# Layer 0 cross attention without wide GpSimd work, pair attention with sums from columns of ones, layer norms on ScalarE

## The chip, the cores and the metric

The kernel runs on one core of a Trainium2 chip. The metric is the device time of one execution in microseconds (us). A core has five engines that run side by side and meet through semaphores: TensorE (PE in the profile, its weight loads PEld), VectorE (DVE), ScalarE (ACT), GpSimd (POOL) and SyncE (SP), which issues most DMAs. Each engine takes its own instructions in order.

## The reference, cut to what matters

A four-layer network on x of shape (16, 64, 256), so 1024 tokens of 256 features, with a context of (16, 1601, 256). Each layer has a cross attention, a self attention and a feed forward block, each on a layer norm of x and added to x. The change touches three of the twelve blocks and every norm.

```
def _layernorm(x, axis=-1, eps=1e-05):
    m = jnp.mean(x, axis=axis, keepdims=True)
    v = jnp.var(x, axis=axis, keepdims=True)
    return (x - m) / jnp.sqrt(v + eps)
...
x = x + _L0_xattn_ref(_layernorm(x, axis=-1), ctx_1024, ctx_1024, mask)
x = x + _L0_attn_ref(_layernorm(x, axis=-1), ...)
...
x = x + _L1_attn_ref(_layernorm(x, axis=-1), ...)
```

Layer 0 cross attention has 16 heads of 16 features over 1601 keys, with a mask that is added to the scores, and a softmax. Layer 0 self attention has 16 heads of 16 over the 64 tokens of a batch element, causal, with a softmax. Layer 1 self attention is linear attention with a feature map elu + 1: its weights are products of q and k, masked causally, and each row is divided by its sum plus 1e-6.

## The kernel before, in words

x stays in SBUF as eight tiles of 128 tokens (two batch elements each); `xn` holds its layer norm. The twelve blocks are the stages of `run`, one after the other. A Tile scheduler orders the instructions of each engine, except those that `pinned` keeps in the order in which the program writes them (while `self.fixed` is set). Weights of the next stage and the context are fetched on SP's queue.

**Norms.** Wherever a tile of x is finished, `ready(t)` runs: L299 and L301 compute mean and variance on VectorE, L303 adds the epsilon on VectorE, L304 takes the power -0.5 on GpSimd. `normalise`, called for the tile before at the next `ready` and once more at the end of a stage, writes xn on VectorE (L311, 128x256). There are 96 of each in a run. In several stages `add_bias` (L350, GpSimd, 128x256) then adds an output bias to x, once xn has been read from it.

**Layer 0 cross attention.** The work is cut into 32 units: 16 batch elements, each with two halves kc of the features (eight heads). A unit has four chunks of 384, 384, 384 and 449 keys. A step n of the main loop does `scores` of one chunk, `lower` of the chunk four steps back, `values` of the chunk six back and `turn` of the chunk five back. `scores`: four matmuls `s` of 32 rows each, into four single-buffered PSUM banks, and on VectorE four L447 that add the mask `mneg`, keep a running maximum and write `Sx`. After the fourth chunk L454 and L457 give the maximum m and its negative. `lower` subtracts m from the four planes of `Sx`: two planes on VectorE (L470), one on ScalarE (L465), one on GpSimd (L466). `turn` transposes them on TensorE (L199, three PSUM buffers `pst`) and takes the exponential on ScalarE (L491; L484 for the 65 keys of the tail, in the last chunk). `values` multiplies by the context with a column of ones into `acc`. `prepare(b)` for the next batch element runs in the first step of each second unit: it issues the context and the mask DMAs, turns the mask from uint8 to -10000 on GpSimd (L419, 128x1601) and masks q on VectorE (L423). Once in two batch elements `back` transposes and divides, and `ready` follows.

**Self attention of layers 0 and 1.** `pair_values` computes V for each tile with V's head columns spread with zeros: 64 x 64-token matmuls, one for each half of the partitions, and L917 adds the bias. The attention loop over eight tiles is a pipeline: `scores` (matmuls into `S4`, then VectorE; in layer 0 also L1037 on GpSimd and an exponential), in layer 0 `turn`, then `values`, then `out`. `values` calls `pair_attend`: 16 matmuls with V as the stationary side give the attention transposed, 8 matmuls with the constant `own` give each head's sum repeated over 32 partitions, a reciprocal of 128x256 on VectorE (L1094, L1092), and a product L1096 that gives `aT`. `out` projects aT (`py`), adds to x (L357) and calls `ready`.

Of the kernel before, what the change touches and what calls it, by code (L numbers as in the profile page):

```python
# [8 lines left out]
F32 = mybir.dt.float32  # L9
# [7 lines left out]
P = 128  # L17
# [27 lines left out]
def _constants():  # L45
# [21 lines left out]
    put("par", ((p[:, None] // 16) % 2) == np.arange(2)[None, :])  # L67
    put("half", (p[:, None] // S) == np.arange(2)[None, :])
    put("iota8", np.broadcast_to(np.arange(8), (P, 8)))
    put("pow", np.broadcast_to(np.array([-0.5, 0.5]), (P, 2)))  # L70
    put("cadd", np.where(same & (p[None, :] <= p[:, None]), 0.0, -1.0e30))
    put("own", (p[:, None] // S) == (np.arange(32)[None, :] // 16))
    put("cadd64", np.where(np.arange(S)[None, :] <= p[:, None] % S, 0.0, -1.0e30))
    put("hd8", ((p[:, None] // 16) == np.arange(8)[None, :]) / S)
    put("neg1", -np.ones((P, 1)))
# [98 lines left out]
class Net:  # L174
# [119 lines left out]
    def ready(self, t):  # L294


        nc, x = self.nc, self.x[:, t, :]
        st = self.stat.tile([P, 6], F32, tag="bst", name="bst")
        nc.vector.bn_stats(st, x)  # L299
        mv = self.stat.tile([P, 2], F32, tag="mv", name="mv")  # L300
        nc.vector.bn_aggr(mv, st)  # L301
        rs = self.stat.tile([P, 1], F32, tag="rs", name="rs")
        nc.vector.tensor_scalar(rs, mv[:, 1:2], 1e-5, None, ALU.add)  # L303
        nc.gpsimd.tensor_tensor(rs, rs, self.c("pow")[:, 0:1], ALU.pow)  # L304
        self.normalise()
        self.due = t, mv, rs

    def normalise(self):
        if self.due is not None:
            t, mv, rs = self.due  # L310
            self.nc.vector.tensor_scalar(  # L311
                self.xn[:, t, :], self.x[:, t, :], mv[:, 0:1], rs, ALU.subtract, ALU.mult
            )
            self.due = None

# [74 lines left out]
    def L0_xattn(self, _):  # L390
# [4 lines left out]
        with (  # L395
# [5 lines left out]
            with (  # L401
# [8 lines left out]
                units = [(b, kc) for b in range(B) for kc in range(2)]  # L410
                state, pairs = {}, {}

                def prepare(b):
                    cn, cT = self.load_ctx(b, "ctx_ones")
                    m8 = sp.tile([P, S2], U8, tag="m8", name="m8", bufs=1)
                    nc.sync.dma_start(m8[0:S], self.io["mask0"][b])
                    nc.sync.dma_start(m8[S:P], self.io["mask0"][b])
                    mneg = sp.tile([P, S2], F32, tag="mneg", name="mneg")
                    nc.gpsimd.tensor_scalar(mneg, m8, -10000.0, 1.0, ALU.mult, ALU.mult)  # L419

                    q = sp.tile([P, 2, 2, S], F32, tag="q", name="q")
                    for i in range(2):
                        nc.vector.tensor_scalar(  # L423
                            q[:, :, i, :], xnT[:, :, b * S : (b + 1) * S],
                            self.c("hm2")[:, i : i + 1], None, ALU.mult,
                        )
                    for kc in range(2):
                        state[2 * b + kc] = dict(b=b, kc=kc, cn=cn, cT=cT, mneg=mneg, q=q, S=[])

                def scores(u, c):  # L430

# [20 lines left out]
                    if c == 3:  # L452
                        m = small.tile([P, 4], F32, tag="m", name="m")
                        nc.vector.tensor_reduce(m, st["mx"], AX.X, ALU.max)  # L454
                        st["m"] = m
                        st["neg"] = small.tile([P, 1], F32, tag="neg", name="neg")
                        nc.vector.tensor_scalar(st["neg"], m[:, 2:3], -1.0, None, ALU.mult)  # L457

                def lower(u, c):

                    st = state[u]
                    n = CHUNKS[c][1]
                    Sj = [st["S"][c][:, j, :n] for j in range(4)]
                    m = st["m"]
                    self.pinned(nc.scalar.activation(Sj[2], Sj[2], AF.Identity, bias=st["neg"]))  # L465
                    nc.gpsimd.tensor_tensor(  # L466
                        Sj[3], Sj[3], m[:, 3:4].to_broadcast([P, n]), ALU.subtract
                    )
                    for j in range(2):
                        self.pinned(nc.vector.tensor_scalar(  # L470
                            Sj[j], Sj[j], m[:, j : j + 1], None, ALU.subtract
                        ))
# [68 lines left out]


                N = 4 * len(units)
                prepare(0)
                for n in range(N + 9):
                    if n < N:
                        scores(*divmod(n, 4))
                        if n % 8 == 4 and n // 8 + 1 < B:
                            prepare(n // 8 + 1)
                    if 0 <= n - 4 < N:  # L550
                        lower(*divmod(n - 4, 4))
                    if 0 <= n - 6 < N:
                        values(*divmod(n - 6, 4))
                    if 0 <= n - 5 < N:
                        turn(*divmod(n - 5, 4))
                    t, i = divmod(n - 7, 16)
                    if i == 15 and t >= 0:
                        back(t)
                    t, i = divmod(n - 8, 16)
                    if i == 15 and t >= 0:  # L560
                        self.ready(t)
# [335 lines left out]
    def pair_values(self, pool, pp, xT, w, bias):  # L897


        nc = self.nc  # L900
        n, k = w.shape[1], xT.shape[0]
        V = pool.tile([P, B, 8, 2, 16], F32, tag="V", name="V")
        nc.gpsimd.memset(V, 0.0)
        bias = bias.rearrange("p (a i f) -> p a i f", i=2, f=16)
        for t in range(NT):
            ps = self.psum(pp, [P, 2, 8, 2, 16], "pst")
            for i in range(2):
                b = 2 * t + i
                for kc in range(n):
                    for r in (slice(0, S), slice(S, P)):  # L910
                        self.mm(
                            ps[r, i].rearrange("p a i f -> p (a i f)"),
                            xT[:, kc, b * S : (b + 1) * S], w[:k, kc, :], kc == 0, kc == n - 1,
                        )
            for i in range(2):
                r = slice(i * S, (i + 1) * S)
                self.pinned(nc.vector.tensor_tensor(  # L917
                    V[r, 2 * t : 2 * t + 2, :, i, :], ps[r, :, :, i, :],
                    bias[r, :, i, :].unsqueeze(1).to_broadcast([S, 2, 8, 16]), ALU.add,
                ))  # L920
        return V.rearrange("p b a i f -> p b a (i f)")

    def L0_attn(self, w):

        nc, tc = self.nc, self.tc
# [1 line left out]
        with (  # L929
# [78 lines left out]
            with (  # L1008
# [42 lines left out]
                    state[t] = PT  # L1051

                def values(t):
                    state[t] = self.pair_attend(sp, psa, V, state[t], t, 0.0)

                def out(t):
                    py = self.psum(psa, [P, D], "py")
# [1 line left out]
                        self.mm(py, state[t][:, kc, :], wo[:, kc, :], kc == 0, kc == 1)  # L1059
                    self.finish_x(t, py)  # L1060

                for n in range(NT + 4):
                    if n < NT:
                        scores(n)
                    if 0 <= n - 4 < NT:
                        out(n - 4)
                    if 0 <= n - 3 < NT:
                        values(n - 3)
                    if 0 <= n - 2 < NT:
                        turn(n - 2)  # L1070
                self.fixed = False

    def pair_attend(self, sp, psa, V, PT, t, eps):


        nc = self.nc
        acc = self.psum(psa, [P, 2, 2, P], "acc")
        for kc in range(2):
            for b in range(2):
                for j in range(4):  # L1080
                    self.mm(
                        acc[32 * j : 32 * j + 32, 0, kc, b * S : (b + 1) * S],
                        V[:, 2 * t + b, 4 * kc + j, :], PT[:, 2 * j + kc, b * S : (b + 1) * S],
                    )
            for j in range(4):
                self.mm(
                    acc[32 * j : 32 * j + 32, 1, kc, :], self.c("own"), PT[:, 2 * j + kc, :]
                )
        rec = sp.tile([P, 2, P], F32, tag="rec", name="rec")
        if eps:  # L1090
            self.pinned(nc.vector.tensor_scalar(rec, acc[:, 1], eps, None, ALU.add))
            self.pinned(nc.vector.reciprocal(rec, rec))  # L1092
        else:
            self.pinned(nc.vector.reciprocal(rec, acc[:, 1]))  # L1094
        aT = sp.tile([P, 2, P], F32, tag="aT", name="aT")
        self.pinned(nc.vector.tensor_tensor(aT, acc[:, 0], rec, ALU.mult))  # L1096
        return aT

    def elu1_T(self, sp, out, ps, bias, shape):
# [11 lines left out]
    def L1_attn(self, w):  # L1111
# [6 lines left out]
        with tc.tile_pool(name="l1a", bufs=1) as wk:  # L1118
# [32 lines left out]
            with (  # L1151
# [24 lines left out]
                    state[t] = A.rearrange("p j (c b) q -> p (j c) (b q)", b=2)  # L1176

                def values(t):
                    state[t] = self.pair_attend(sp, psa, V, state[t], t, 1e-6)

                def out(t):
                    py = self.psum(psa, [P, D], "py")
# [1 line left out]
                        self.mm(py, state[t][:, kc, :], wout[:, kc, :], kc == 0, kc == 1)  # L1184
                    self.finish_x(t, py)

                for n in range(NT + 2):
                    if n < NT:
                        scores(n)
                    if 0 <= n - 2 < NT:  # L1190
                        out(n - 2)
                    if 0 <= n - 1 < NT:
                        values(n - 1)
                self.fixed = False
# [937 lines left out]
```

## Time and profile before

| | |
|---|---|
| time, median of 3 runs | 3475.49 us (3474.08 to 3479.93) |
| the profiled execution, its own time | 3481.06 us |
| its span, first to last instruction | 3479.3 us |
| mean granted TensorE clock | 0.942 |
| TensorE, VectorE, ScalarE, GpSimd busy | 3170.8, 1387.8, 1065.1, 470.1 us |
| layer 0 cross attention | up to about 558 us |
| layer 0 self attention | about 558 to 657 us |
| layer 1 self attention | about 1856 to 1950 us |

The stage limits are read from the lines that write x at a stage's end (L536 at 557.56, L304 at 656.79, L357 at 1855.52 and 1949.52). The profiled execution is one run with the profiler on, 5.6 us above the median of the runs without it. Busy time is that of an engine's instructions; TensorE's matmuls overlap, and a matmul that is held up inside a group can make the group look longer, so a busy TensorE is not one at its peak.

### The profile page before, as it was taken

The page shows a single profiled execution, that of the slowest core. Times are in us where ns is not written, and L with a number is a line of the kernel's source. Part 1 is how long each engine was busy: PE and PEld are TensorE (multiplying, and loading weights), DVE is VectorE, ACT ScalarE, POOL GpSimd, SP SyncE. Part 2 cuts the span into 40 slices and gives each one's busy share as a digit, 9 for nine tenths or more (in the row PEclk, how much of TensorE's full clock was granted, in tenths as well). Part 3 has the DMA queues.
Part 4 walks back from the last instruction along what each step waited for, and adds up shares of the span by engine and source line. Part 5 has one row for each costly group of instructions (what it writes and reads, how often), then busy time and mean ns, then how long its engine had stood idle before and what let it go on. Part 6 is the DMA issues. An engine that isn't in the chain of part 4 may idle for free.

```text
span 3479.3 us, 69200 instructions
## 1 busy us (share of the span) xinstructions
PE 3170.8 (91%) x29623; PEld 2365.5 (68%) x29623; DVE 1387.8 (40%) x3702; ACT 1065.1 (31%) x2191; POOL 470.1 (14%) x478
## 2 busy tenths in 40 slices
PE   7999998699899999999998689999987978888798
PEld 4666664499566666666665367777766966767697
DVE  6888885622333333333334862222234010126300
ACT  3555654111112111212111112222221367753111
POOL 2333222222100000000000000000001311110132
PEclk9999998699899999999998699999997979998899
DMA  6333331389011112111139001111114835520297
GB/s 198 103 126 124 94 115 58 122 289 320 17 58 56 57 57 76 38 60 55 57 113 308 15 13 57 57 57 57 38 53 162 273 123 179 187 88 1 107 324 246
DMA packets 178368, 395.12 MB, mean 114 GB/s; under 512 B 11446, under 2 KB 142270, under 8 KB 165214
## 3 DMA queue, kind: packets, MB, share of 16 engines
q1 hardware_dynamic: 165070, 372.81, 31.2%
q0 software_dynamic: 11712, 16.00, 2.3%
q8 instruction: 234, 3.83, 0.5%
q10 hardware_dynamic: 1280, 1.89, 0.2%
q14 instruction: 72, 0.59, 0.1%
HBM read 374.94 MB, written 16.12 MB: 112 GB/s over the span
## 4 chain that ended last, share of the span: by engine, by line
PE 77%; DVE 11%; DMA 5%; issue 5%; POOL 1%; ACT 1%; SPq 0%; POOLq 0%; ACTq 0%; DVEq 0%
PE acc L195 16%; PE pss L195 15%; PE pst L195 13%; PE pst L199 9%; PE pso L195 5%; PE psk L195 5%; PE s L195 4%; PE p L195 4%; DMA l3o<-y,token 3%; PE ps L195 3%; PE psh L195 2%; DVE Sx L447 2%; DVE Sx L470 1%; POOL rs L304 1%; PE py L195 1%
## 5 line engine op out<-in xcount | busy, mean ns | idle before, releaser
L199 PE MATMUL pst<-cst,Sx 128*128 128x128 f32 (+1 forms) x2568 | 377.7, 286 | 42.9 <-DVE Sx L470 14.1
L195 PE MATMUL pss<-ctxT,qk 128*128 128x512 f32 (+1 forms) x1024 | 403.3, 519 | 0.0
L199 PEld LDWEIGHTS pst<-cst,Sx 128*128 128x128 f32 (+1 forms) x2568 | 287.9, 144 | 167.0 <-issue 70.2
L195 PE MATMUL acc<-ctx,PT 128*128 128x256 f32 (+1 forms) x1664 | 374.0, 382 | 0.0
L195 PEld LDWEIGHTS acc<-ctx,PT 128*128 128x128 f32 (+1 forms) x1664 | 314.1, 192 | 40.2
L447 DVE CUSTOM_DVE_ANT_0 Sx<-s,mneg 128x384 f32<-128x384 f32 (+1 forms) x512 | 262.7, 567 | 79.0 <-PE s L195 69.8
L304 POOL TENSOR_TENSOR rs<-rs,cst 128x1 f32<-128x1 f32 x96 | 57.4, 600 | 1602.3 <-DVE rs L303 1495.4
L491 ACT ACTIVATE PT<-pst 128x384 f32<-128x384 f32 x512 | 221.3, 489 | 154.1 <-PE pst L199 152.8
L824 ACT ACTIVATE Pr<-pss 128x512 f32<-128x512 f32 (+1 forms) x512 | 220.4, 523 | 68.8 <-PE pss L195 67.3
L376 ACT ACTIVATE Sx<-Sx,nm 128x1601 f32<-128x1601 f32 x64 | 104.4, 1631 | 432.2 <-DVE nm L630 432.2
L195 PEld LDWEIGHTS pss<-ctxT,qk 128*128 128x128 f32 x1024 | 160.9, 190 | 79.3 <-issue 72.3
L195 PE MATMUL pso<-W,hT 128*128 128x256 f32 x884 | 200.9, 379 | 0.0
L195 PE MATMUL pst<-wst,ctxT 128*128 128x256 f32 (+1 forms) x832 | 183.4, 381 | 0.0
L195 PE MATMUL psk<-ctxT,wst 128*128 128x512 f32 (+1 forms) x512 | 181.8, 513 | 0.8 <-ACT qT L686 0.8
L195 PEld LDWEIGHTS pso<-W,hT 128*128 128x128 f32 x884 | 163.3, 190 | 19.6
L195 PEld LDWEIGHTS pst<-wst,ctxT 128*128 128x128 f32 (+1 forms) x832 | 153.6, 186 | 25.8 <-issue 2.7
L195 PE MATMUL pss<-q,ctxT 32*128 32x128 f32 (+1 forms) x3328 | 151.3, 300 | 16.6 <-issue 13.9
L195 PE MATMUL s<-ctxT,q 32*128 32x384 f32 (+1 forms) x1024 | 160.2, 572 | 6.3 <-DVE mx L447 4.9
L625 DVE TENSOR_SCALAR_CACHE_REDUCE Sx<-pss 128x1024 f32<-128x1024 f32 (+1 forms) x128 | 127.0, 992 | 82.6 <-PE pss L195 82.6
L640 DVE TENSOR_SCALAR Z<-acc,rec 128x256 f32<-128x256 f32 x64 | 31.0, 484 | 322.6 <-PE acc L195 322.6
L195 PEld LDWEIGHTS pss<-q,ctxT 32*128 32x128 f32 (+1 forms) x3328 | 119.4, 194 | 48.5 <-issue 39.5
L195 PEld LDWEIGHTS psk<-ctxT,wst 128*128 128x128 f32 x512 | 88.3, 190 | 93.6 <-issue 92.0
(387 smaller groups left out, 4479.1 us busy)
## 6 DMA issues: line engine op xcount, KB each, us to landing
ctxT<-in_ctxT_dram SPq DMA_DIRECT2D x64, 1601.0 KB
ctx<-in_ctx_dram SPq DMA_DIRECT2D x48, 1536.0 KB
W<-in_L_experts_dram SPq DMA_DIRECT2D x61, 1024.0 KB
W<-in_L_experts_dram SPq DMA_DIRECT2D x23, 1536.0 KB
ctx<-in_ctx_ones_dram SPq DMA_DIRECT2D x16, 1632.0 KB
W<-in_L_experts_dram SPq DMA_DIRECT2D x23, 768.0 KB
W<-in_L_experts_dram SPq DMA_DIRECT2D x15, 1028.0 KB
m<-in_mask_dram SPq DMA_DIRECT2D x32, 100.1 KB
```

What stands on the lines that cost most here:

```text
L195: self.pinned(self.nc.tensor.matmul(out, lhsT, rhs, start=start, stop=stop))
L199: self.pinned(self.nc.tensor.transpose(out, in_, self.ident[:n, :n]))
L304: nc.gpsimd.tensor_tensor(rs, rs, self.c("pow")[:, 0:1], ALU.pow)
L376: nc.scalar.activation(Sx, Sx, AF.Exp, bias=bias, scale=scale, accum_out=total)
L447: self.pinned(nc.vector.tensor_tensor_reduce(out=Sx[:, j, :n], in0=ps[j][:, :n], in1=st["mneg"][:, o : o + n], op0=ALU.add, op1=ALU.max, s ...
L470: self.pinned(nc.vector.tensor_scalar(Sj[j], Sj[j], m[:, j : j + 1], None, ALU.subtract))
L491: self.pinned(nc.scalar.activation(PT, ps, AF.Exp))
L625: nc.vector.tensor_scalar(Sx[:, o : o + n], ps[:, :n], HD**-0.5, None, ALU.mult, ALU.max, accum_out=mx[:, h : h + 1],)
L640: nc.vector.tensor_scalar(Z, acc, rec, None, ALU.mult)
L824: nc.scalar.activation(st["Pr"][:kn, g : g + n, j, :], ps[j][:kn, :n, :], AF.Silu)
```

## The change

It does five things. In `lower`, the fourth plane goes from GpSimd to ScalarE, which now lowers two planes. `prepare` is split: `fetch(b)` issues the DMAs (the mask first, then the context) at the start of the first step of a batch element's predecessor, and `prepare(b)` keeps its step but runs after `turn`, with the mask's conversion on ScalarE instead of GpSimd, and is pinned. `pair_values` uses whole 128-token matmuls and stores V with two more columns for each head pair, 1 for one head's rows and 0 for the other's (34 columns). `pair_attend` makes the probabilities the stationary side, so that attention and sums come out by token, the reciprocal is on 128x16, and a new pipeline stage `back` transposes the result (two transposes, one copy on ScalarE). In the norm the epsilon, the power and minus mean times rs are three GpSimd instructions of 128x1, and xn is written by ScalarE.

```
-        rs = self.stat.tile([P, 1], F32, tag="rs", name="rs")
-        nc.vector.tensor_scalar(rs, mv[:, 1:2], 1e-5, None, ALU.add)
-        nc.gpsimd.tensor_tensor(rs, rs, self.c("pow")[:, 0:1], ALU.pow)
         self.normalise()
-        self.due = t, mv, rs
+        rs = self.stat.tile([P, 2], F32, tag="rs", name="rs")
+        nc.gpsimd.tensor_tensor(rs[:, 0:1], mv[:, 1:2], self.c("eps"), ALU.add)
+        nc.gpsimd.tensor_tensor(rs[:, 0:1], rs[:, 0:1], self.c("pow")[:, 0:1], ALU.pow)
+        nc.gpsimd.tensor_scalar(rs[:, 1:2], mv[:, 0:1], rs[:, 0:1], -1.0, ALU.mult, ALU.mult)
+        self.due = t, rs
...
-            self.nc.vector.tensor_scalar(
-                self.xn[:, t, :], self.x[:, t, :], mv[:, 0:1], rs, ALU.subtract, ALU.mult
+            self.nc.scalar.activation(
+                self.xn[:, t, :], self.x[:, t, :], AF.Identity, bias=rs[:, 1:2], scale=rs[:, 0:1]
             )
...
-                def prepare(b):
-                    cn, cT = self.load_ctx(b, "ctx_ones")
+                def fetch(b):
                     m8 = sp.tile([P, S2], U8, tag="m8", name="m8", bufs=1)
                     nc.sync.dma_start(m8[0:S], self.io["mask0"][b])
                     nc.sync.dma_start(m8[S:P], self.io["mask0"][b])
+                    cn, cT = self.load_ctx(b, "ctx_ones")
...
+                def prepare(b):
                     mneg = sp.tile([P, S2], F32, tag="mneg", name="mneg")
-                    nc.gpsimd.tensor_scalar(mneg, m8, -10000.0, 1.0, ALU.mult, ALU.mult)
+                    self.pinned(nc.scalar.activation(
+                        mneg, state[2 * b]["m8"], AF.Copy, scale=-10000.0
+                    ))
...
-                    self.pinned(nc.scalar.activation(Sj[2], Sj[2], AF.Identity, bias=st["neg"]))
-                    nc.gpsimd.tensor_tensor(
-                        Sj[3], Sj[3], m[:, 3:4].to_broadcast([P, n]), ALU.subtract
-                    )
+                    for j in range(2, 4):
+                        self.pinned(nc.scalar.activation(
+                            Sj[j], Sj[j], AF.Identity, bias=st["neg"][:, j - 2 : j - 1]
+                        ))
...
-        V = pool.tile([P, B, 8, 2, 16], F32, tag="V", name="V")
+        V = pool.tile([P, NT, 2, 8, 34], F32, tag="V", name="V")
         nc.gpsimd.memset(V, 0.0)
+        for i in range(2):
+            nc.gpsimd.memset(V[i * S : (i + 1) * S, :, :, :, 32 + i], 1.0)
...
+            for u in range(2):
                 for kc in range(n):
-                    for r in (slice(0, S), slice(S, P)):
-                        self.mm(
-                            ps[r, i].rearrange("p a i f -> p (a i f)"),
-                            xT[:, kc, b * S : (b + 1) * S], w[:k, kc, :], kc == 0, kc == n - 1,
-                        )
+                    self.mm(
+                        ps[:, u].rearrange("p a i f -> p (a i f)"),
+                        xT[:, kc, (t + u) * P : (t + u + 1) * P], w[:k, kc, :],
+                        kc == 0, kc == n - 1,
+                    )
...
-    def pair_attend(self, sp, psa, V, PT, t, eps):
+    def pair_attend(self, sp, acc, V, PT, t, eps):
...
+        for a in range(8):
             for b in range(2):
+                r = slice(b * S, (b + 1) * S)
+                self.mm(acc[r, a, :], PT[:, 2 * (a % 4) + a // 4, r], V[:, t, b, a, :])
+        rec = sp.tile([P, 8, 2], F32, tag="rec", name="rec")
...
+            self.pinned(nc.vector.reciprocal(rec, acc[:, :, 32:34]))
+        att = sp.tile([P, 8, 2, 16], F32, tag="att", name="att")
+        self.pinned(nc.vector.tensor_tensor(
+            att, acc[:, :, :32].rearrange("p a (i f) -> p a i f", f=16),
+            rec.unsqueeze(3).to_broadcast([P, 8, 2, 16]), ALU.mult,
+        ))
...
+    def pair_back(self, sp, ps, att):
+        for kc in range(2):
+            self.tr(ps[:, kc, :], att[:, kc * P : (kc + 1) * P])
         aT = sp.tile([P, 2, P], F32, tag="aT", name="aT")
-        self.pinned(nc.vector.tensor_tensor(aT, acc[:, 0], rec, ALU.mult))
+        self.pinned(self.nc.scalar.copy(aT, ps))
         return aT
...
-                for n in range(NT + 4):
+                for n in range(NT + 5):
                     if n < NT:
                         scores(n)
+                    if 0 <= n - 5 < NT:
+                        out(n - 5)
                     if 0 <= n - 4 < NT:
-                        out(n - 4)
+                        back(n - 4)
```

Layer 1's loop changes in the same way: `out` three steps back, `back` two, `values` one, so NT + 3 steps instead of NT + 2.

## The prediction

> **What bounds the kernel now.** I read the page first, for the shares of the engines, then the timeline and busy time by windows inside the three stages that the change rewrites, because an average over twelve stages says nothing on them.
>
> ```profile
> PE 3170.8 (91%) x29623; PEld 2365.5 (68%) x29623; DVE 1387.8 (40%) x3702; ACT 1065.1 (31%) x2191; POOL 470.1 (14%) x478
> core 0: us, PE busy (x) PEld busy (x) DVE busy (x) ACT busy (x) POOL busy (x), PEclk, DMA share, GB/s
> 200.00:264.00 64.00, 61.31 (x1173) 42.31 (x1172) 55.11 (x182) 37.84 (x85) 20.27 (x21) 1.00 0.36 115
> 1917.00:1924.00 7.00, 5.93 (x92) 4.49 (x92) 5.22 (x10) 0.00 (x0) 0.55 (x1) 0.50 0.01 2
> ```
>
> TensorE looks like the bound everywhere, also at 200 to 264 us (layer 0 cross attention, 96% busy) and in one step of layer 1's attention loop (1917 to 1924), there at half its clock. The timeline says otherwise:
>
> ```profile
> 200.09 0.93 PE L195 MATMUL s<-ctxT,q 32*128 32x384 f32 x8
> 200.36 3.18 DVE L470 TENSOR_SCALAR Sx<-Sx,m 128x449 f32<-128x449 f32 x4
> 200.43 3.90 POOL L466 TENSOR_TENSOR Sx<-Sx,m 128x384 f32<-128x384 f32 x4 [9.64 <-ACT PT L491]
> ...
> 204.07 2.34 PE L195 MATMUL s<-ctxT,q 32*128 32x384 f32 x8
> ...
> 207.28 0.74 DVE L470 TENSOR_SCALAR Sx<-Sx,m 128x384 f32<-128x384 f32 x2
> ...
> 209.10 0.93 PE L195 MATMUL s<-ctxT,q 32*128 32x384 f32 x8
> ...
> 212.50 1.04 PE L195 MATMUL s<-ctxT,q 32*128 32x449 f32 x8
> ```
>
> Columns are start and duration. Two L470 take 0.74 alone, but four take 3.18 while GpSimd runs its four L466 of a unit in one go. The next `s` group then needs 2.34 instead of 0.93, since each of its matmuls waits for VectorE to empty a bank: TensorE is "busy" while held up. In the self attention the loop runs through VectorE:
>
> ```profile
> 1917.44 1.75 DVE L1092 RECIPROCAL rec<-rec 128x256 f32<-128x256 f32 x1
> 1919.22 0.42 DVE L1096 TENSOR_TENSOR aT<-acc,rec 128x256 f32<-128x256 f32 x1
> 1919.56 1.21 DVE L1171 TENSOR_TENSOR A<-S,cst 128x1024 f32<-128x1024 f32 x1
> 1919.70 1.35 PEld L195 LDWEIGHTS py<-wst,aT 128*128 128x128 f32 x4 [1.26 <-DVE aT L1096]
> 1919.70 2.07 PE L195 MATMUL py<-wst,aT 128*128 128x256 f32 x4 [1.07 <-DVE aT L1096]
> DVE xn L311 <- POOL rs L304: 41.8, 65, 2.6
> ```
>
> `py` waits for `aT`, that for the reciprocal, that for `acc`, which stands behind `py` in TensorE's queue: a ring of 6.92 us. The last line, from the view of waits, is the norm: VectorE idles 41.8 us in all for GpSimd's power.
>
> **What the Trainium skill says.** "GPSIMD Engine Reference", Key points: GpSimd shares its SBUF interfaces with VectorE, with contention for VectorE instructions in a 2-port mode or with two SBUF inputs. The trace agrees: L470, one input from SBUF, is 0.418 us in the median and 1.101 at most. "ScalarE: Activation LUTs", What ACT_TABLE_LOAD costs: an activation takes 186 ns plus 0.833 ns an element plus about 93 ns for each pointer operand. For L465 (384 columns, one pointer) that is 0.60; the trace shows 0.61. "TensorE: Matmul & The Clock Gate", What's actually happening: TensorE's clock is half or full, by how busy it has lately been. The trace shows 0.50 at 1917 and 1.00 at 200.
>
> **The parts, in us; minus is a gain.**
>
> *Layer 0 cross attention, planes.* Starts of `s` from the timeline: 200.09, 204.07, 209.10, 212.50, 216.00, 221.14, 224.76, 228.15, 231.66. The steps are 3.98, 5.03, 3.40, 3.50 for one unit and 5.14, 3.62, 3.39, 3.51 for the next. Without hold-ups the four kinds take 3.98, 3.62, 3.39, 3.50: 14.49. A batch element (two units) loses 1.42 and 1.18: the first by L466 beside L470, the second by L466, L419 and the q products (L423: four in 1.78, at 0.28 each otherwise 1.1). 16 x 2.6 = 41.6 to win. VectorE then needs, in a unit, sixteen L447 (12 x 0.48 + 4 x 0.545 from start to start), L470 3.1, maximum 0.3, q and copies 0.5: 11.8 of 14.5; it isn't the bound.
> What ScalarE gets: 128 more Identity of about 0.62, and 16 mask copies, which by the page's price are 186 + 0.833 x 1601 ns = 1.52 (estimate). A step on ScalarE: in the step from 209.10 L465 starts at 209.65 and the first L491 at 211.41; two Identity 0.56 apart end at 210.82, 0.59 before it. They are hidden. Their wait for L457 ends 0.35 into a unit's first step, before ScalarE has come so far. The mask copy is not hidden: it stands behind the exponentials of the unit's first step (end 204.61 in a step that starts at 200.09), so it ends at 206.1 and the two Identity at 207.3; the exponentials of the next step could start at 206.5. They come 0.7 late, and as `pst` has three buffers the fourth group of transposes waits for the first exponential: 0.7 x 16 = +11. Together -30. Bounds: no cost for the copy, -41; half of the hold-up has another cause, with 1.2 a batch for the copy as well, -5.
> The DMAs: the mask now stands ahead of the context on SP's queue, and the context's second tensor still waits for its slot until the sixth step. They are issued no later than before, and 3.3 MB in some 30 us at 115 GB/s leave nothing to wait for: 0.
> *Start.* L447 began at 28.15, after L419 (26.58), which waited for the mask behind the context. Now the mask is there early, and the end is set by norms: eight tiles of 1.1 on GpSimd (below) from 12.75, then xn, transposes, copy and mask copy, about 25.7: -2.5 (0 to -4).
>
> *Layer 0 self attention.* VectorE was 9.53 of 10 us busy at 620 to 630. A tile loses the reciprocal 1.75, L311 (0.41, up to 1.97 beside L1037) and L303 0.15, and gets a reciprocal of 128x16, 0.26 by L525. What stays: 1.23 + 1.22 + 0.47 + 0.46 + 0.2 + 0.26 + 0.43 = 4.3 against about 6. TensorE: scores 0.69, `py` 1.06, transposes 0.3, `turn` 1.05, and the new `values`, which no row shows: 32 records with 64 columns loaded and 34 streamed. Two halves side by side as in `pair_values` (0.11 a record) and shorter: 1.1 (0.9 to 1.7); 4.2 in all at the full clock. Four full steps gain 1.7 each, and the draining steps, which now are 4.74 for the reciprocal ring, about 3.5 to 1.5; the added stage costs one short step of about 2. Walked from the first `s` at 596.3 the last add to x comes at about 643 instead of 654.9: -12 (-5 to -17). `pair_values` gains nothing here: L917 still is 16 x 0.43 on VectorE, which ended it.
>
> *Layer 1 self attention.* `pair_values`: before 128 records in 14.1 us, in front of VectorE. Now 32 of about 0.25: 8; VectorE's 16 x 0.43 after the k products (1879.1) end at 1886.5 instead of 1891.1: -4.5. The loop: the ring opens, TensorE alone is left. At the half clock scores 1.99 + `py` 2.0 + transposes 0.5 + `values` 2.0 = 6.5 against 6.92; at the full clock 1.12 + 1.06 + 0.3 + 1.1 = 3.6, with VectorE then at 3.5. I take the half clock: the loop still begins with `s` and A in turns, as at 1891 to 1895, where the clock fell. The last two steps, 6.92 each before, become some 4.5 and 5: -8 (+4 to -20). Together -12.5.
>
> *Norms.* GpSimd rows give the price by two sizes: TENSOR_TENSOR 0.73 at 256 and 1.90 at 1024 columns, so 0.34 at one; TENSOR_SCALAR 0.41 at 256 and 1.53 at 1601, so 0.20. The chain is 0.34 + 0.55 + 0.20 = 1.1 on GpSimd for 0.15 + 0.55; xn is 186 + 2 x 93 + 213 ns = 0.59 on ScalarE for 0.41 (estimates). So +0.6 where the next stage waits for the last tile. That is so at nine ends; at two of them V's memset (3.5 now, 6% longer, with two small ones) stands ahead as well, +1: 6.5. Where eight tiles come at once (892 to 905, with L350 between; 2791 to 2799) GpSimd's queue is the limit: +3 and +1.2. Inside stages a norm lies beside TensorE. New waits: xn stands in ScalarE's queue for GpSimd's chain, with exponentials behind it, but is written only at the next tile's `ready`, when the chain is long done; L350 on GpSimd waits for xn, and the next chain stands behind L350, which is why the packed ends cost more. Sum +11 (+6 to +18).
>
> Sum: -30 - 2.5 - 12 - 12.5 + 11 = **-46** on the profiled 3481.1 us (span 3479.3 and 1.8 around it), so 3435; that execution is 5.6 above the median of the runs shown, so **3429.5** as a median.
>
> **Rivals.**
> 1. *TensorE is the bound in layer 0 cross attention.* For it: 96% busy. Against: the 2.34 for a 0.93 group. Then that stage gains nothing: -16, 3459. Chance 0.08.
> 2. *ScalarE becomes the bound there: slower.* The two Identity stand ahead of each step's exponentials. Up to 0.59 us a step is free; beyond, each us delays the fourth group in 128 steps. The gain of 46 is gone when the pair overruns by 0.36 (0.95 later than I have it); at 0.45, +12: 3487. Against: 13 us of ScalarE work for a unit of 14.5. Chance 0.05.
> 3. *Layer 1's loop runs at the full clock:* 12 more, 3418; *or its `values` is slow (3.4 at the half clock):* 11 less, 3440. Inside the range; counted with the forecast.
> 4. *Norms eat the rest:* if each of 96 cost its 0.6, 58 instead of 11, the total is zero: 3476. Against: GpSimd idles 1495 us ahead of L304. Chance 0.02.
>
> **Chances and range.** The forecast with rival 3 has 0.85. The ends come from the bounds, which don't fall together: 3403 to 3456. Two tenths of a per cent, 7 us, is about what a measurement of this kernel can tell from no change. Faster 0.92, same 0.02, slower 0.06.
>
> **What would show it.** L470 near 0.42 throughout; `s` groups 0.93 in every step and a unit near 14.5 to 14.9; exponentials late only behind the mask copy; L1092's successor near 0.26; the clock in layer 1's loop; xn on ScalarE about 0.6 after a chain of 1.1. Steps of 5 us in layer 0 cross attention, or exponentials that start after the fourth group of transposes is due, would make it wrong.

## The result, and the profile after

The changed kernel takes 3439.03 us in the median of four runs (3438.02 to 3449.11), the kernel before 3477.71 beside it (3474.08 to 3483.61): a ratio of 0.9904, 95% interval 0.9886 to 0.9923. The forecast was 3429.5, with a range of 3403 to 3456. The profiled execution has a span of 3437.1 us, 42.2 less than before, where the sum said 46; by the medians the gain is 38.7, since the profiled execution of before lay 3.4 above its median. The total is nearly right, but its terms are not. The table compares, by the last power of a norm in each stage, how long the stages take in the profile:

| stage | before | after | difference | predicted |
|---|---|---|---|---|
| layer 0 cross attention, with the start | 561.8 | 551.5 | -10.3 | -32.5 |
| layer 0 self attention | 95.0 | 91.9 | -3.1 | -12 |
| layer 1 self attention | 96.8 | 72.5 | -24.3 | -12.5 |
| all others together | 2725.7 | 2721.2 | -4.5 | +11 (norms) |

The page's busy times of after:

```profile
PE 3129.4 (91%) x29255; PEld 2348.1 (68%) x29255; DVE 1260.8 (37%) x3510; ACT 1202.7 (35%) x2447; POOL 370.7 (11%) x530
```

TensorE's share hasn't moved; as before, it tells nothing here. Busy time by windows, one pair of batch elements of layer 0 cross attention and one stretch of layer 1's loop (columns as shown before):

```profile
173.00:237.00 64.00, 58.88 (x1172) 41.59 (x1172) 48.12 (x182) 48.68 (x103) 2.94 (x7) 0.97 0.36 119
1899.00:1906.00 7.00, 7.00 (x118) 5.78 (x114) 6.13 (x16) 1.95 (x4) 2.10 (x7) 1.00 0.02 7
```

In layer 0 cross attention GpSimd is down from 20.27 to 2.94 and VectorE from 55.11 to 48.12, yet TensorE does the same work (1172 matmuls, 1173 before) in the same 64 us: the hold-ups went, and something else took their place. The timeline where the first pair ends names it (start, duration; the brackets give the idle time before and who ended it):

```profile
106.12 1.03 PE L195 MATMUL s<-ctxT,q 32*128 32x449 f32 x8
110.52 0.63 POOL L307 TENSOR_SCALAR rs<-mv,rs 128x1 f32<-128x1 f32 x1
111.19 0.60 ACT L313 ACTIVATE xn<-x,rs 128x256 f32<-128x256 f32 x1 [3.79 <-POOL rs L307]
111.69 1.23 ACT L499 ACTIVATE PT<-pst 128x384 f32<-128x384 f32 x3
112.21 0.50 PEld L199 LDWEIGHTS pst<-cst,Sx 128*128 128x128 f32 x3 [3.36 <-ACT PT L499]
113.05 1.66 PE L195 MATMUL s<-ctxT,q 32*128 32x384 f32 x8
117.95 0.93 PE L195 MATMUL s<-ctxT,q 32*128 32x384 f32 x8
```

xn of the first tile (L313) stands in ScalarE's queue directly behind its own norm. It waits 3.79 us for GpSimd's chain. The exponentials (L499) stand behind it, the transposes need a PSUM buffer that the exponentials empty, and `s` stands behind the transposes. The step takes 6.93 instead of 3.44. The next `s` group takes 1.66 instead of 0.93, at half the clock (0.50 granted from 112 to 115 us), and that step 4.90. It happens seven times; for the tile xn the profile gives 25.4 us of waiting in seven instructions.

What was wanted of the subtractions did come: L478, the old L470, takes 0.417 in the median and 0.458 at most (before: 1.101), and away from xn the steps of a unit without a mask copy are 3.88, 3.56, 3.33 and 3.44, so 14.21.

In layer 1 self attention the ring is open and the clock is full:

```profile
1898.29 0.25 DVE L1102 RECIPROCAL rec<-rec 128x16 f32<-128x16 f32 x1
1899.02 1.13 PE L195 MATMUL py<-wst,aT 128*128 128x256 f32 x4
1901.35 1.12 PE L195 MATMUL S<-qT,k 32*128 32x64 f32 x32
1902.40 1.13 PE L195 MATMUL py<-wst,aT 128*128 128x256 f32 x4
```

`py` comes every 3.38 us instead of 6.92, the reciprocal takes 0.25 instead of 1.75, and TensorE is busy for all of the 7.00 us.

### The profile page after: what moved, and what is told of

Read it like the earlier page. It is cut to its first block, busy times and chain, and to the rows that moved or that the text cites. A ratio compares the mean times of both kernels' runs of the same rounds, so it can differ in the third digit from the quotient of the medians.

```text
span 3437.1 us, 68480 instructions
## 1 busy us (share of the span) xinstructions
PE 3129.4 (91%) x29255; PEld 2348.1 (68%) x29255; DVE 1260.8 (37%) x3510; ACT 1202.7 (35%) x2447; POOL 370.7 (11%) x530
## 4 chain that ended last, share of the span: by engine, by line
PE 79%; DVE 6%; issue 5%; DMA 3%; ACT 3%; POOL 2%; POOLq 0%; ACTq 0%; DVEq 0%
PE acc L195 17%; PE pss L195 15%; PE pst L195 13%; PE pst L199 9%; PE pso L195 6%; PE psk L195 5%; PE p L195 4%; PE s L195 3%; PE ps L195 3%; PE psh L195 3%; DMA l3o<-y,token 2%; POOL rs L306 1%; ACT PT L499 1%; ACT mneg L425 1%; PE S L195 1%
## 5 line engine op out<-in xcount | busy, mean ns | idle before, releaser
L499 ACT ACTIVATE PT<-pst 128x384 f32<-128x384 f32 x512 | 215.3, 489 | 57.6 <-PE pst L199 55.7
L305 POOL TENSOR_TENSOR rs<-mv,cst 128x1 f32<-128x1 f32 x96 | 20.3, 211 | 1582.4 <-DVE mv L301 1526.3
L474 ACT ACTIVATE Sx<-Sx,neg 128x384 f32<-128x384 f32 (+1 forms) x256 | 146.4, 621 | 11.3 <-DVE neg L465 11.2
```

The costliest lines, as they stand in the source:

```text
L305: nc.gpsimd.tensor_tensor(rs[:, 0:1], mv[:, 1:2], self.c("eps"), ALU.add)
L474: self.pinned(nc.scalar.activation(Sj[j], Sj[j], AF.Identity, bias=st["neg"][:, j - 2 : j - 1]))
L499: self.pinned(nc.scalar.activation(PT, ps, AF.Exp))
```

## The experiments

Theory A: in layer 0 cross attention xn, free to be placed by the scheduler, stands at the head of ScalarE's queue while GpSimd's chain is under way. Rival B: the planes and the mask copy that ScalarE was given are too much in themselves. Rival C: TensorE is the bound. Rival D: norms on ScalarE cost nothing, or gain where VectorE is the bound; the prediction had them cost where a stage ends. The length of a pair is the mean of six pairs, from one attention added to x to the next.

**The norms as before, in the changed kernel.** `ready` and `normalise` of the kernel before:

```
-            self.nc.scalar.activation(
-                self.xn[:, t, :], self.x[:, t, :], AF.Identity, bias=rs[:, 1:2], scale=rs[:, 0:1]
+            self.nc.vector.tensor_scalar(
+                self.xn[:, t, :], self.x[:, t, :], mv[:, 0:1], rs, ALU.subtract, ALU.mult
```

> The changed kernel (3439.0 us), with the layer norms of the kernel before: epsilon and xn on VectorE, the power alone on GpSimd. Theory A, xn stands at the head of ScalarE's queue in layer 0 cross attention while GpSimd's chain is under way and costs some 5.4 us in each of seven pairs of batch elements: 38 us come back there, and some 5 more at the stage ends where the norm is waited for, so 3396 (3386 to 3406); the pair of batch elements takes about 58.6 us instead of 64.0. Rival B, the two Identity and the mask copy on ScalarE hold layer 0 cross attention up: the pair stays at 64 and only the stage ends come back, 3431 (3426 to 3436). Rival C, TensorE bounds that stage: as B.

Measured: 3415.2 us (3412.8 to 3418.2), ratio to before 0.9822 (0.9805 to 0.9838). A pair takes 59.6 instead of 63.7, and layer 0 cross attention ends 32.3 earlier. That is A; B and C are out. The miss of 19 against the expectation has mostly two parts: the pair gives back 4.1 and not 5.4, and layer 0 self attention is 6.6 longer (98.5), which is taken up below.

**xn kept in the program's order, in the changed kernel.**

```
-            self.nc.scalar.activation(
+            self.pinned(self.nc.scalar.activation(
                 self.xn[:, t, :], self.x[:, t, :], AF.Identity, bias=rs[:, 1:2], scale=rs[:, 0:1]
-            )
+            ))
```

> The changed kernel (3439.0 us), with xn kept in the order in which the program writes it, so that in layer 0 cross attention it stands one tile (64 us) behind its own chain instead of directly behind it; every instruction stays. Theory A (xn waits at the head of ScalarE's queue, 5.4 us in each of seven pairs): 3401 (3393 to 3411), a little above the kernel with the norms of before, since the stage ends still pay. Rival B (the work that ScalarE was given is too much in itself): 3439 within 4, because ScalarE still does all of it. Rival C (TensorE is the bound): 3439.

Measured: 3411.3 us (3406.1 to 3412.9), ratio 0.9808 (0.9791 to 0.9826). The same instructions, 28 us less. Its timeline at the end of the second pair:

```profile
165.25 1.04 PE L195 MATMUL s<-ctxT,q 32*128 32x449 f32 x8
168.69 1.40 PE L195 MATMUL s<-ctxT,q 32*128 32x384 f32 x8
169.25 0.59 ACT L313 ACTIVATE xn<-x,rs 128x256 f32<-128x256 f32 x1
169.67 0.35 POOL L307 TENSOR_SCALAR rs<-mv,rs 128x1 f32<-128x1 f32 x1
173.02 0.93 PE L195 MATMUL s<-ctxT,q 32*128 32x384 f32 x8
```

L313 here writes the tile of the pair before and starts while the new chain is still going on (L307 at 169.67): it waits for nothing, and the step from 165.25 takes 3.44. A pair takes 59.1. ScalarE does all the work that rival B blames. In this stage the granted clock was 0.50 for 3.4 to 6.8 us behind each of the seven waits of after; with xn pinned it was 1.00 throughout.

**The norms alone, in the kernel before.** The diff's lines of `ready` and `normalise` only:

```
+            self.nc.scalar.activation(
+                self.xn[:, t, :], self.x[:, t, :], AF.Identity, bias=rs[:, 1:2], scale=rs[:, 0:1]
+            )
```

> The kernel before (3477.7 us) with the change of the norms alone. xn again stands directly behind its chain in layer 0 cross attention's ScalarE queue. Theory A: that costs 3 to 5 us in each of seven pairs, 20 to 38, and the stage ends cost 6 to 18 more: 3515 (3500 to 3530). Rival B (norms on ScalarE cost only at the stage ends): 3489 (3484 to 3496). Rival D (norms cost nothing, or are a gain where VectorE is the bound): 3474 to 3479.

Measured: 3496.4 us (3490.9 to 3496.8), ratio 1.0058 (1.0041 to 1.0075): 0.6% slower, and below the range of theory A. The pair takes 68.5 instead of 64.2, and layer 0 cross attention ends 23.7 later. The whole run is only 20.6 longer by the medians, so the rest of it is some 3 us shorter, not 6 to 18 longer (in the profiles it is 14 shorter, but this profiled execution lies 5.5 below its median and that of before above). That no cost shows outside one stage only rival D allowed for.

**The norms alone in the kernel before, xn pinned,** by the edit shown above.

> The kernel before (3475 to 3477 us) with the change of the norms alone, and xn kept in program order on ScalarE. With xn free, that change alone took 3496 us. Theory A (all that the norms cost is where xn stands in ScalarE's queue in layer 0 cross attention; elsewhere the work taken from VectorE pays for the longer chain): 3462 to 3474, and 58 to 64 us for a pair of batch elements instead of 68.4. The prediction's term for the norms (+11 at stage ends): 3487. Rival G (ScalarE has no room for xn wherever it stands): 3494 to 3498.

Measured: 3467.9 us (3459.1 to 3470.0), ratio 0.9965 (0.9952 to 0.9977). The norms that cost 20.6 are a gain of 11.4 once xn doesn't wait; the pair takes 62.9, and layer 0 cross attention ends 11.4 earlier, so by the medians the other stages together neither gain nor lose. Rival G is out, and so is the prediction's +11.

**Layer 0 cross attention alone, in the kernel before.** The diff's lines of `fetch`, `prepare`, `scores` and `lower` only:

```
+                    for j in range(2, 4):
+                        self.pinned(nc.scalar.activation(
+                            Sj[j], Sj[j], AF.Identity, bias=st["neg"][:, j - 2 : j - 1]
+                        ))
```

> The kernel before (3477.7 us) with the change of layer 0 cross attention alone: both Identity and the mask copy on ScalarE, norms and self attentions as before. Theory A: no xn on ScalarE, so the whole gain of the planes shows: a pair takes some 58.5 us instead of 64.2, eight pairs, so 3432 (3424 to 3442). Rival B (the ScalarE work eats the gain): 3467 to 3477. Rival C (TensorE is the bound): 3477.

Measured: 3441.4 us (3434.4 to 3445.1), ratio 0.9895 (0.9875 to 0.9916). The pair takes 59.5, and the stage ends 44.0 earlier in the profile, as A has it; 4.5 us of that are gone by the end of the run, in stages that this kernel doesn't change, and for which no cause was looked for.

**The self attentions alone, in the kernel before.** The diff's lines of `pair_values`, `pair_attend`, `pair_back` and the two loops only:

```
+                    if 0 <= n - 4 < NT:
+                        back(n - 4)
```

> The kernel before (3475.7 to 3477.7 us) with the change of the two self attentions alone; norms and layer 0 cross attention as before. Theory A (read from the stages of the runs so far): layer 0's stage gains nothing, because the copy of aT stands behind the exponential in ScalarE's queue (95 us before, 95 to 99 here), and layer 1's gains 24 to 27 (96.8 before, 70 to 73 here), because it runs at the full clock: 3452 (3446 to 3457). The prediction's own terms, -12 in each stage (83 and 84), give the same sum, 3452, so it is the two stages that tell. Rival B (layer 1's gain came from the norms on ScalarE): layer 1's stage above 85, total 3465.

Measured: 3455.2 us (3453.4 to 3470.3), ratio 0.9947 (0.9933 to 0.9961). Both readings give the sum; the stages decide: layer 0's takes 97.7 (before 95.0), layer 1's 69.6 (before 96.8). So layer 1 gave all, with the norms of before, and layer 0 lost a little. The three parts alone sum to -35.5 (20.6 - 34.3 - 21.8) against -38.7 for the change as a whole.

Why layer 0's loop gains nothing is in the timeline of after, one step of it:

```profile
603.94 1.15 PE L195 MATMUL S<-k,qT 32*64 32x128 f32 x32
607.91 1.90 POOL L1050 TENSOR_TENSOR Sx<-Sx,mx 128x1024 f32<-128x1024 f32 x1 [5.64 <-DVE rec L1104]
609.85 1.06 ACT L1053 ACTIVATE Sx<-Sx 128x1024 f32<-128x1024 f32 x1 [5.22 <-POOL Sx L1050]
610.81 0.35 ACT L1117 COPY aT<-pst 128x256 f32<-128x256 f32 x1
611.22 0.72 PEld L199 LDWEIGHTS pst<-cst,Sx 128*128 128x128 f32 x4 [3.00 <-ACT aT L1117]
612.26 1.16 PE L195 MATMUL S<-k,qT 32*64 32x128 f32 x32
```

`back` takes one of the two `pst` buffers, and its copy L1117 stands behind the exponential of the newest tile, which waits for GpSimd's subtraction, VectorE's maximum and mask addition, and `S`. The second half of `turn` waits for that buffer, and the next `S` stands behind `turn`: a new ring of 8.3 us. For the last two exponentials of after the scheduler had put the copies ahead (aT at 622.20, exponential at 625.59), and the step fell to 4.0; with xn pinned it didn't, and that stage is 7.5 longer there: one more step of 8.4 instead of 4.0, and a drain some 3 longer.

**The exponential behind the copies.** From the kernel with xn pinned, the exponential leaves `scores`:

```
+                def soft(t):
+                    Sx = state[t]
+                    self.pinned(nc.scalar.activation(Sx, Sx, AF.Exp, scale=0.25))
...
                     if 0 <= n - 2 < NT:
                         turn(n - 2)
+                    if n < NT:
+                        soft(n)
```

> The changed kernel with xn kept in program order (3411.3 us), and in layer 0 self attention the exponential of a tile written after aT's copy and the two copies of turn of the same step, not before them. No instruction is added or removed. Theory A: the ring of about 8.2 us (scores, mask add, maximum, subtraction on GpSimd, exponential, then aT's copy, which frees the PSUM buffer for turn) opens; steps of 4 to 5.5 us; the stage takes 80 to 84 us instead of 99.4, so 3394 (3389 to 3400). Rival B: TensorE at half clock bounds the loop (about 7 us of work in a step): the stage takes 92 to 97, 3406. Rival C: the order of the norms, not the exponential, made these steps long: 3411.

Measured: 3391.5 us (3386.2 to 3397.6), ratio 0.9750 (0.9731 to 0.9769). The stage takes 78.5 instead of 99.4:

```profile
569.57 0.69 PE L195 MATMUL S<-k,qT 32*64 32x128 f32 x32
570.96 1.06 ACT L1057 ACTIVATE Sx<-Sx 128x1024 f32<-128x1024 f32 x1 [0.70 <-POOL Sx L1050]
571.92 0.35 ACT L1123 COPY aT<-pst 128x256 f32<-128x256 f32 x1
573.54 0.69 PE L195 MATMUL S<-k,qT 32*64 32x128 f32 x32
```

`S` comes every 4.0 us. The exponential ahead of aT's copy belongs to the tile before and is ready in time, and TensorE reaches the full clock.

**The fourth plane back on GpSimd.** From the kernel with xn pinned:

```
-                    for j in range(2, 4):
-                        self.pinned(nc.scalar.activation(
-                            Sj[j], Sj[j], AF.Identity, bias=st["neg"][:, j - 2 : j - 1]
-                        ))
+                    self.pinned(nc.scalar.activation(
+                        Sj[2], Sj[2], AF.Identity, bias=st["neg"][:, 0:1]
+                    ))
+                    nc.gpsimd.tensor_tensor(
+                        Sj[3], Sj[3], m[:, 3:4].to_broadcast([P, n]), ALU.subtract
+                    )
```

> The changed kernel with xn kept in program order (3411.3 us), with the fourth plane of lower back on GpSimd; the mask copy stays on ScalarE. Theory A (wide GpSimd work beside VectorE was what held the units up, the prediction's first step): 1.4 to 2.6 us for each of 16 batch elements come back, so 3434 to 3453, with VectorE's subtractions up to 1.1 us again instead of 0.42. Rival B (the gain came from fetching and preparing in another order): 3411 within 4, or less, as ScalarE is given 75 us less work.

Measured: 3415.4 us (3412.8 to 3417.1), ratio 0.9826 (0.9808 to 0.9843). The prediction's first step fails here, as far as the fourth plane goes. VectorE's subtractions do stretch to 1.11 us beside GpSimd, but the pair stays at 59.1 and the whole run is 4 us longer, where 23 to 42 were expected. (The pair is a sum of small gains and losses: with one Identity less on ScalarE one mask copy in two costs nothing, 3.62 instead of 4.00 for the step behind it, while three steps of a unit are 0.06 longer.) What else had changed? In the trace of before, VectorE in one unit of two runs four L470 in a row (the 3.18 shown with the prediction) ahead of eight L447; in every trace with the new `prepare` it runs two subtractions, four mask additions, two subtractions. Theory E: that order and the contention cost only together.

**`prepare` behind `turn` and nothing else, in the kernel before.** Its q products are pinned; plane, mask, norms and self attentions stay as before:

```
-                        if n % 8 == 4 and n // 8 + 1 < B:
-                            prepare(n // 8 + 1)
...
                         turn(*divmod(n - 5, 4))
+                    if n % 8 == 4 and n // 8 + 1 < B:
+                        prepare(n // 8 + 1)
```

> The kernel before (3476 us), with one thing from the change of layer 0 cross attention: prepare is called after turn and its two q products keep their program order, so that VectorE runs each chunk's subtractions behind the next chunk's four mask additions in every unit (in the kernel before, one unit in two has two pairs of subtractions in a row ahead of eight mask additions). The fourth plane and the mask's conversion stay on GpSimd, norms and self attentions as before. Theory E (that order of VectorE made the long steps, and only together with GpSimd's wide work): a pair of batch elements takes 59 to 61 us instead of 64.2, total 3432 to 3452. Theory P (the prediction's: GpSimd's wide work beside VectorE holds TensorE up, whatever the order): 64 stays, 3472 to 3480.

Measured: 3449.9 us (3444.5 to 3454.5), ratio 0.9925 (0.9908 to 0.9941). With all of GpSimd's work in place the pair takes 60.7:

```profile
188.97 0.93 PE L195 MATMUL s<-ctxT,q 32*128 32x384 f32 x8
189.24 1.38 DVE L470 TENSOR_SCALAR Sx<-Sx,m 128x449 f32<-128x449 f32 x2
189.31 3.68 POOL L466 TENSOR_TENSOR Sx<-Sx,m 128x384 f32<-128x384 f32 x4 [9.63 <-ACT PT L491]
192.45 1.08 DVE L470 TENSOR_SCALAR Sx<-Sx,m 128x384 f32<-128x384 f32 x2
192.82 0.93 PE L195 MATMUL s<-ctxT,q 32*128 32x384 f32 x8
```

Two subtractions beside GpSimd take 1.38 instead of 0.8, but the four mask additions follow in time, so both steps (3.85 from 188.97, then 3.62 to 196.44) are as short as without contention. Not every step is. In the first step of a batch element the mask's conversion (L419) runs beside two subtractions:

```profile
263.94 0.93 PE L195 MATMUL s<-ctxT,q 32*128 32x384 f32 x8
263.99 1.53 POOL L419 TENSOR_SCALAR mneg<-m 128x1601 f32<-128x1601 uint8 x1 [10.41 <-DVE mx L447]
264.21 2.48 DVE L470 TENSOR_SCALAR Sx<-Sx,m 128x449 f32<-128x449 f32 x2
266.75 2.15 PE L199 MATMUL pst<-cst,Sx 128*65 128x128 f32 x15 [0.54 <-DVE Sx L470]
268.83 0.93 PE L195 MATMUL s<-ctxT,q 32*128 32x384 f32 x8
```

They take 2.48, the transposes wait for them, and this step takes 4.89. In the kernel above with the fourth plane alone on GpSimd, the first step of a pair takes 3.86 (4.89 here; medians of six pairs).

**The old order without wide GpSimd work.** The kernel with xn pinned, `prepare` back in its old place and its q products free:

```
                         scores(*divmod(n, 4))
+                        if n % 8 == 4 and n // 8 + 1 < B:
+                            prepare(n // 8 + 1)
...
                         turn(*divmod(n - 5, 4))
-                    if n % 8 == 4 and n // 8 + 1 < B:
-                        prepare(n // 8 + 1)
```

> The changed kernel with xn kept in program order (3411.3 us), with prepare back in its old place ahead of lower and its q products free again, so that VectorE has the order of the kernel before (one unit in two with two pairs of subtractions ahead of eight mask additions); both Identity and the mask copy stay on ScalarE, nothing wide is on GpSimd. Theory E (order and GpSimd's wide work only cost together): the four subtractions take 1.7 instead of 3.2, and the pair of batch elements stays at 58 to 61 us, 3405 to 3425. Theory F (the order alone costs): 62 to 65, 3435 to 3460. Theory P: 59, 3411.

Measured: 3412.6 us (3407.0 to 3417.5), ratio 0.9824 (0.9806 to 0.9842), the pair 59.2.

```profile
182.79 0.95 PE L195 MATMUL s<-ctxT,q 32*128 32x384 f32 x8
183.09 1.47 DVE L478 TENSOR_SCALAR Sx<-Sx,m 128x449 f32<-128x449 f32 x4
187.26 0.93 PE L195 MATMUL s<-ctxT,q 32*128 32x384 f32 x8
```

Here are the four in a row again, in 1.47 instead of 3.18, and the next `s` group takes 0.93. With the other kernels there is enough to compare like with like. A pair of batch elements takes, in us:

| order on VectorE, and the norms | wide work on GpSimd | none |
|---|---|---|
| four subtractions in a row in one unit of two, norms on VectorE | 64.2 (before) | |
| the same, norms on ScalarE, xn pinned | 62.9 | 59.2 |
| two at a time in every unit, norms on VectorE | 60.7 | 59.5 |
| the same, norms on ScalarE, xn pinned | | 59.1 |

E is shown for most of it: taking GpSimd's work away wins 3.7 in the old order and 1.2 in the new one, and the new order wins 3.5 beside GpSimd's work and 0.1 without it. Either half of the edit takes most of the gain, and together they add little. As the plane back on GpSimd left the pair at 59.1, the 1.2 of the new order do not come from the plane; the step of 4.89 points to the mask's conversion, which was not moved by itself. One more thing differs between the columns: all kernels of the right one also issue the DMAs earlier (`fetch`). That was not run alone either, but in the trace of before there was little to win: from 100 to 480 us, waits that a DMA ended are 3.8 us in all, seven of about 0.5 on weight loads.

**The mask in four pieces.** From the kernel with the exponential behind the copies, one piece in each of four steps:

```
-                    self.pinned(nc.scalar.activation(
-                        mneg, state[2 * b]["m8"], AF.Copy, scale=-10000.0
-                    ))
...
+                    r = slice(CHUNKS[c][0], sum(CHUNKS[c]))
+                    self.pinned(nc.scalar.activation(
+                        st["mneg"][:, r], st["m8"][:, r], AF.Copy, scale=-10000.0
+                    ))
...
+                    if n % 8 >= 4 and n // 8 + 1 < B:
+                        mask(n // 8 + 1, n % 8 - 4)
```

> The kernel with the exponential behind the copies (3394 expected), with the mask of a batch element converted in four pieces of 384 to 449 keys in four steps instead of one piece of 1601. Three more instructions for each of 15 batch elements, about 0.2 us each. Theory A: a piece of some 0.5 us fits in the 0.6 us that a step leaves on ScalarE, so the 0.45 us that the whole copy costs in its step go: 7 us less than the kernel with the exponential behind the copies. Rival B (a step has no room on ScalarE): the pieces cost their time, 0 to 10 us more.

Measured: 3384.2 us (3383.9 to 3392.8), ratio 0.9743 (0.9722 to 0.9763). Layer 0 cross attention ends 7.6 earlier in the profile, and the pair takes 58.1, as expected; the two ranges overlap. This is the fastest of all kernels: 93 us (2.6%) below the kernel before on the same chip, where the change as made gives 39.

## Why the prediction was right or wrong

*Sign and total: right.* -42.2 in the profile for -46. It is right by luck, by errors that cancel: some 22 too much gain in layer 0 cross attention and 9 too much in layer 0 self attention, against 12 too little in layer 1 and some 16 in the norms elsewhere (12 if all that the profiles show beyond the medians lies there).

*Layer 0 cross attention, the size: too small once xn is out of the way.* The term was -32.5 with the start; with xn pinned the stage ends 43.5 earlier, 5.1 a pair instead of some 3.8. A unit without hold-ups takes 14.21 and not 14.49: three of its steps are 0.06 shorter once the fourth plane has left GpSimd (with the plane back there they are 3.62, 3.40 and 3.50 again), and its first is 0.1 shorter. The mask copy costs less too. Over 32 units and 16 copies that is some 9 and 4 us, about the miss. ScalarE keeps up: the Identity takes 0.608 (0.60 by the price in the Trainium skill, "ScalarE: Activation LUTs", What ACT_TABLE_LOAD costs), the mask copy 1.537 (1.52) and xn 0.600 (0.59). The copy costs 0.45 a batch element, not 0.7: a second step of 4.00 with it and 3.56 without. So rival 2, ScalarE as the bound through the Identity, is wrong as it was put; what did hold ScalarE up was xn in the same queue, which it didn't name. Rival 1, TensorE as the bound, is out: with xn pinned the same matmuls take 59.1 instead of 64.2 a pair.

*Layer 0 cross attention, the cause: half right.* The prediction charged L466 beside L470 with 1.42 a batch element, and put no price on the new place of `prepare`. The contention is real, but beside L466 it reached TensorE only through the order of four subtractions ahead of eight mask additions. The step that failed is reading the cost from one unit without asking why the other unit of the same batch element, with the same L466, loses its time in another step. The other loss, 1.18 charged to L466, L419 and the q products, stands better: beside L419 a step is about 1.0 longer in the new order too.

*The norms: wrong in sign and place.* The step that failed is the sentence that xn "is written only at the next tile's `ready`, when the chain is long done". That is the order of the program. The instruction isn't pinned, and in the trace of after the first one in this stage's loop runs at 111.19, directly behind its chain; pinned, the same tile's is written at 169.25, a pair later. It cost 4.6 a pair, 33.2 by the end of the stage; the term said 0 there and +11 at the stage ends. Rival 4 priced the norms as a sum over 96 and missed a single wait with a queue behind it. What the prediction asked a reader to look for, exponentials later than the fourth group of transposes, is what was seen.

*Layer 0 self attention: wrong.* -3.1 for -12, and +2.7 with this part alone. The step that failed is the list of a step's work: it had TensorE's and VectorE's shares, but not the copy of aT in ScalarE's queue, nor that `back` takes one of the two buffers of `turn`. Behind the exponential they make a ring of 8.3 where the walk had steps of some 4.2; with the exponential behind the copies they are 4.0. `values` itself was priced well: 1.13 at the full clock and 1.93 at the half (1.1 and 2.0).

*Layer 1 self attention: the direction right, the size twice as large.* Rival 3 holds: the clock goes full during the loop, at 1890.3, and a step then takes 3.38 (3.6 was worked out). The term mis-sized is the loop, about -21 for -8. The choice of half clock came from a loop whose ring starved TensorE; with the ring gone, the steps at half clock filled it (busy for all of 1880 to 1890 us at 0.50). That agrees with what the prediction quoted from the Trainium skill, "TensorE: Matmul & The Clock Gate", What's actually happening: the clock follows how busy TensorE has lately been.

*The start:* the first mask addition begins at 26.99 instead of 28.15, so -1.2 for -2.5; the mask is ready at 25.65, as worked out, but the first `s` group takes 1.66 and ends at 26.87.

## What to carry to other kernels

An instruction that moves to another engine takes its wait with it: ask what stands behind it in that queue, and if a scheduler may place it, look up its place in the built order, not in the program. A copy that frees a shared PSUM buffer belongs ahead of work that waits for another engine. And a hold-up read from a trace can need two things at once, contention and an order; test each alone before you pay for removing both.

## What the runs showed of the hardware

Contention goes both ways: GpSimd's third norm instruction of 128x1 (L307) took 0.26 us alone and 0.35 to 0.70 while VectorE's subtractions ran beside it (in the changed kernel and with xn pinned). A stall of 3.4 us on TensorE costs more than itself: the matmuls after it ran at half the clock (1.66 instead of 0.93 for a group). And VectorE's work can grow by half, 1.38 instead of 0.81 for two subtractions beside the plane's subtraction, with no effect on a step; at 2.48, beside the mask's conversion, it did have one.
